# Cross-attention in 16 batches: the 64-row products of two batches in one row, sums ahead of additions, Wq loaded and turned in halves

## The chip, the cores and the metric

The kernel runs on one core of one Trainium2 chip. The metric is the device time of one execution in microseconds (us). The kernel before has a median of 275.02 us in 3 runs (274.48 to 275.05).

## The reference

One cross-attention layer with 8 heads of width 256, all in float32: 16 batches of 256 rows of `x` (256 wide) attend to 77 rows of a context (192 wide), and a residual and a layer norm follow.

```python
Q = (x @ Wq), K = (c @ Wk), V = (c @ Wv)      # each split into 8 heads of 256
score = einsum('bhqd,bhkd->bhqk', Q, K) / sqrt(256)
score = where(mask, score, -inf)
attn = softmax(score)
ctx = einsum('bhqk,bhkd->bqhd', attn, V).reshape(B, 256, 8 * 256)
out = ctx @ Wo + x
return (out - mean(out)) * rsqrt(var(out) + 1e-5) * gamma + beta
```

## The kernel before

**Algebra.** Nothing of size Q, K or V is formed. A prologue works out, for each head, `g = Wk Wq^T / 16` (tiles gA, gB) and `u = Wv Wo` (uA, uB). Then a batch needs `a = g^T c^T` (so that the scores are `x a`) and `vw = c u` (so that the output is the sum over heads of attn times vw).

**128 rows and 64 rows.** The context is 192 wide, so each of these products is a sum over 128 rows (part A, operands cA, gA, uA) and over 64 rows (part B, operands cB, gB, uB, in which two 64-row products run side by side). `prepare_a` (line 153) and `prepare_vw` (line 198) return three functions: part_A and part_B, which issue matmuls into the same PSUM tiles, part A with start and part B with stop, and copies, a list of what is then to be copied to SBUF. prepare_a makes, in each step, one pair of heads of the a of a *group* of four batches (the next group's); prepare_vw makes the vw of one batch. In the last group the a is made in halves of two batches, spread over the steps of batches 10 to 13.

**PSUM.** All tiles come from one pool of eight slots (ps_mm, tag mm), a slot being a bank. A new tile waits, at its first matmul, for the last reader of the tile whose slot it takes.

**The order.** The schedule is manual: each engine executes its instructions in the order in which the program issues them. The loop from line 882 runs over b = -1 to 14; its body makes the scores and softmax of batch b + 1 (*new*, two tiles of 128 rows), the attention output of batch b (*now*) and the layer norm of batch b - 1 (*old*). I call it "the step of batch b + 1". In the steps up to batch 13 it issues:

- TensorE: scores of the two new tiles (L283, 4 banks); part A of vw and of a (L208, L173), then part B of both (L219, L185), 2 + 4 banks; the products of the batch before (`seven`, L416, banks pm and po), a seven-product scheme of Strassen's kind over two tiles and two halves of the columns.
- Vector engine: for each new tile two additions of the bias (s, L298) and the maximum (top, L305); up to batch 6 a turn of vr (L273); for each tile the old tile's statistics (L471, L474), the softmax sum and its reciprocal (den, L318, L320); normalise of the old tiles (L513, L532) around the transposes of p (L336) and, in two steps of four, of the next group's x (L150); the two additions of po to the output (L463, in `add_seven`).
- Scalar engine: eight exponentials for each tile (L312), two small instructions of the layer norm (L492, L493), the copies of vw and a (L922), the copy of pm to m (L439).
- GpSimd: p = e times the reciprocal, two instructions per tile (L326); the differences of vw blocks for the next `seven` (L379); `add_seven`'s five additions (L449); the four sums of p blocks for the next `seven` (`sums`, L396 to L399).

The first step (b = -1) has no now and no old, and has a bias for the batches from 4 on to prepare on the Vector engine and GpSimd. The last two steps use plain products (`attend`, L348) in place of seven.

**The prologue.** SP issues all loads of weights in order. `load_blocks` (line 574) loads a block tile with four DMAs, one for each 32 partitions. Wk and Wq of head pairs 1 to 3 come alternately, then Wv, Wo and the rest of the context. `turn_blk` (line 677) transposes a pair's two blocks on the Vector engine in 32 by 32 blocks (L679), `g_of_pair` (L777) and `rest_of_g_of_pair` (L793) multiply them.

Of the kernel before, what the change touches and what calls it, by code (L numbers as in the profile page):

```python
# [8 lines left out]
F32 = mybir.dt.float32  # L9
# [6 lines left out]
P = 128  # L16
# [3 lines left out]
GB = 4  # L20
# [5 lines left out]
def kernel(  # L26
# [13 lines left out]
    nc = tc.nc  # L40
    B, S, DI = x.shape
# [3 lines left out]
    NG = B // GB  # L45
# [3 lines left out]
    NF = H // 2  # L49
    KR = S2 - KM  # L50
    BK = 32
    NM = P // BK
# [97 lines left out]
        nc.vector.transpose(cols, cols)  # L150


    def prepare_a(g, places, lo=0, hi=GB):


        if 0 in places:
            a_of[g] = in_two("a", [P, 2, GB, H, S2], g)
        parts = [
            (2 * u + i, dc) for u in places for dc in range(2) for i in range(2)
        ]  # L160
        batches = slice(g * GB + lo, g * GB + hi)
        banks = [
            ps_mm.tile([P, hi - lo, S2], F32, tag="mm", name=f"pa_{g}_{h}_{dc}_{lo}")
            for h, dc in parts
        ]

        def cols(dc, i):
            return slice((2 * i + dc) * BK, (2 * i + dc + 1) * BK)

        def part_A():  # L170
            for (h, dc), o in zip(parts, banks):
                for i in range(NM):
                    nc.tensor.matmul(  # L173
                        flat(o[i * BK : (i + 1) * BK]),
                        gA[:, h, cols(dc, i)],
                        flat(cA[:, batches, :]),
                        start=True,
                        stop=False,
                    )

        def part_B():
            for j in range(0, len(parts), 2):
                for i in range(NM):
                    for k, (h, dc) in enumerate(parts[j : j + 2]):
                        nc.tensor.matmul(  # L185
                            flat(banks[j + k][i * BK : (i + 1) * BK]),
                            gB[half(k), h // 2, cols(dc, i)],
                            flat(cB[half(k), batches, :]),
                            start=False,
                            stop=True,  # L190
                        )
# [6 lines left out]
    def prepare_vw(b):  # L198

        vw_of[b] = vwp.tile([P, 4, 2, P], F32, tag="vw", name=f"vw_{b}", bufs=3)  # L200
        parts = slice(0, 4) if b < NS else slice(1, 5)
        pv = []

        def part_A():
            for k in range(2):
                pv.append(ps_mm.tile([P, 2 * DI], F32, tag="mm", name=f"pv_{b}_{k}"))
                for i in range(NM):
                    nc.tensor.matmul(  # L208
                        pv[k][i * BK : (i + 1) * BK],
                        cA[:, b, k * BK : (k + 1) * BK],  # L210
                        uA[:, parts, :, i],
                        start=True,
                        stop=False,
                    )

        def part_B():
            for i in range(NM):
                for k in range(2):
                    nc.tensor.matmul(  # L219
                        pv[k][i * BK : (i + 1) * BK],  # L220
                        cB[half(k), b, k * BK : (k + 1) * BK],
                        uB[half(k), parts, :, i],
                        start=False,
                        stop=True,
                    )
# [89 lines left out]
    def weigh(t):  # L315
        e = e_of.pop(t)
        den = st.tile([P, H], F32, tag="den", name=f"den_{t}")
        nc.vector.tensor_reduce(den, e, AX.X, ALU.add)  # L318
        rden = st.tile([P, H], F32, tag="rden", name=f"rden_{t}")
        nc.vector.reciprocal(rden, den)  # L320
        p = p_ring[t % 2]
        e_mh = e.rearrange("p (m h) k -> p m h k", h=2)
        rden_mh = rden.rearrange("p (m h) -> p m h", h=2)
        for cols, keys in ((slice(2 * KM), slice(KM)), (slice(2 * KM, 2 * S2), slice(KM, None))):
            part = p[:, :, cols].rearrange("p m (h k) -> p m h k", h=2)
            nc.gpsimd.tensor_tensor(  # L326
                part,
                e_mh[:, :, :, keys],
                rden_mh.unsqueeze(3).to_broadcast(list(part.shape)),
                ALU.mult,  # L330
            )
# [226 lines left out]
    with tc.tile_pool(name="wonce", bufs=1) as wp:  # L558
# [12 lines left out]
        wq_rows = wq[:, : 2 * D].rearrange("(t p) f -> p t f", p=P)  # L571
        wk_ends = wk[P:, : 2 * D].rearrange("r (e f) -> r e f", e=2)

        def load_blocks(to, blocks):
            for i in range(NM):
                nc.sync.dma_start(to[i * BK : (i + 1) * BK], blocks[i])


        rest = slice(first * CR, None)
# [24 lines left out]
        nc.sync.dma_start(c_sb, c_rows[:, :first, :])  # L604
        for a in range(1, NF):
            load_blocks(wk_blk[:, a - 1], wk_blocks[a])
            load_blocks(wq_blk[:, a - 1], wq_blocks[a])

        nc.scalar.preload_act_table_set("natural_log_exp_and_others")

# [64 lines left out]
            )  # L675

        def turn_blk(a):
            for blk, of in ((wk_blk, kT_blk), (wq_blk, qT_blk)):
                nc.vector.transpose(  # L679
                    of[a].rearrange("p n (m r) -> p m n r", r=BK),  # L680
                    blk[:, a - 1].rearrange("p m (n c) -> p m n c", c=BK),
                )

        def turn_c():
# [192 lines left out]
    pools[1] = vwp = late  # L877


    assert QT == 2  # L880
    last = NT - 1
    for b in range(-1, B - 1):
        old = range(max(b - 1, 0) * QT, b * QT)
        now = range(max(b, 0) * QT, (b + 1) * QT)
        new = range((b + 1) * QT, (b + 2) * QT)
        for t in new:
            scores(t)
        if b == B - 2:
# [12 lines left out]
        if g < NG - 1 or g == NG - 1 and n < NF // 2:  # L901
            work.append(prepare_a(g, (n,)))
        elif b < NS:
            work.append(prepare_a(NG - 1, (NF // 2 + n % 2,), *((0, 2) if g < NG else (2, GB))))
        for part_A, _, _ in work:
            part_A()
        for _, part_B, _ in work:
            part_B()
        for i, t in enumerate(new):
            exponential(t)  # L910
            if old and b < B - 2:
                finish(old[i])
            weigh(t)
        if old and b < B - 2:
            spread(old[0], old[-1] + 1)
        if b < 0:
            bias_of(GB, B)
            for j in range(GT // 2, GT, 2):
                transpose_x(0, j)
        for _, _, copies in work:  # L920
            for dst, src in copies():
                nc.scalar.copy(dst, src)  # L922
        if b + 1 < NS:
            differences(b + 1)
        if b < NS:
            if now:
                seven(b)
            if old:
                invert(old[0], old[-1] + 1)
                normalise(old[0])  # L930
            for t in new:
                turn(t)
            if g < NG and n >= NF - 2:
                for j in range((n - NF + 2) * GT // 2, (n - NF + 3) * GT // 2, 2):
                    transpose_x(g, j)
            if old:
                normalise(old[1])


            if g < NG and n == NF - 1:  # L940
# [80 lines left out]
```

## Time and profile before

| What | Value |
|---|---|
| median of 3 runs | 275.02 us (274.48 to 275.05) |
| the profiled execution | 274.61 us, of which its span 272.8 us |
| busy TensorE | 97% of the span |
| busy Vector engine / GpSimd / Scalar engine | 78% / 62% / 50% |
| granted TensorE clock | 0.999 |
| chain that ended last | TensorE 89%, DMA 7%, Vector engine 1%, SP's queue 1% |

The span is the time between the first and the last instruction of the profiled execution. PE is TensorE's matmuls, DVE the Vector engine, ACT the Scalar engine, POOL GpSimd, SPq the queue that issues DMAs. A line of the chain has the start, the time it takes in the chain, the engine, the tile and the source line. A line of an engine's timeline has the start, the time from the first start to the last end, the line, the operation, output <- input, shapes, the number of instructions and, in brackets, how long the engine was idle before and what ended that. An instruction's time can overlap the one before it by some hundredths.

### The profile page before, as it was taken

To read this page: it belongs to the slowest core of one execution; us is meant where nothing else is said; L and a number is where in the kernel's file an instruction comes from. 1 tells how busy PE (TensorE), PEld (TensorE's weight loads), DVE (VectorE), ACT (ScalarE), POOL (GpSimd) and SP (SyncE) were. 2 spreads that over 40 slices of the span, in tenths; PEclk is the share of its full clock that TensorE was granted. 3 is DMA by queue.
4 is the path that set the end of the run, shared out by engine and by line. 5 is a ranking of instruction groups with operands and counts; after the bars stand their busy time and mean duration, and the time that the engine had idled before them with its cause. 6 is when DMAs were issued, how large, how long until landed. Compare 5 with 4: busy or idle time off the path is not lost.

```text
span 272.8 us, 14124 instructions
## 1 busy us (share of the span) xinstructions
PE 265.8 (97%) x6312; PEld 194.3 (71%) x6312; DVE 214.1 (78%) x418; ACT 136.2 (50%) x444; POOL 170.4 (62%) x231
## 2 busy tenths in 40 slices
PE   7999999999999999999999999999999999999992
PEld 6557486867494949495959586867796969694662
DVE  0554938589759898979799897878798989889875
ACT  3233225363918182827364646464546372927652
POOL 1000002809887878687878777777788789845754
PEclk9999999999999999999999999999999999999999
DMA  6999989940000322310221405000504061010102
GB/s 191 194 198 189 305 160 183 278 53 2 2 5 4 88 35 73 124 44 4 70 52 36 87 19 180 31 16 9 116 2 120 2 197 41 5 43 4 61 22 77
DMA packets 42460, 22.66 MB, mean 83 GB/s; under 512 B 23632, under 2 KB 41632, under 8 KB 42400
## 3 DMA queue, kind: packets, MB, share of 16 engines
q1 hardware_dynamic: 42400, 21.77, 34.8%
q8 instruction: 49, 0.80, 1.3%
q14 instruction: 11, 0.09, 0.1%
HBM read 17.57 MB, written 4.19 MB: 80 GB/s over the span
## 4 chain that ended last, share of the span: by engine, by line
PE 89%; DMA 7%; DVE 1%; SPq 1%; issue 0%; DVEq 0%
PE ps L283 25%; PE pa L173 11%; PE po L416 10%; PE pv L208 10%; PE pm L416 9%; PE pv L219 6%; PE pa L185 5%; DMA wq_blk<-in_L_xattn_Wq_dram 5%; PE po L348 4%; PE pu L717 3%; PE pr L242 2%; DMA c_sb<-in_ctx_dram 2%; PE pw L731 1%; PE pr L254 1%; PE po L364 1%; PE pgb L777 1%
## 5 line engine op out<-in xcount | busy, mean ns | idle before, releaser
L312 ACT ACTIVATE e<-s,top 128x77 f32<-128x77 f32 x256 | 66.8, 346 | 73.4 <-DVE top L305 73.4
L283 PE MATMUL ps<-a,xT 128*32 128x154 f32 x2048 | 70.0, 294 | 0.0
L326 POOL TENSOR_TENSOR p<-e,rden 128x512 f32<-128x512 f32 x64 | 47.8, 768 | 31.8 <-DVE rden L320 16.6
L283 PEld LDWEIGHTS ps<-a,xT 128*32 128x32 f32 x2048 | 66.0, 110 | 1.5 <-issue 0.8
L298 DVE TENSOR_TENSOR s<-ps,bias 128x308 f32<-128x308 f32 x64 | 29.7, 473 | 14.7 <-PE ps L283 14.6
L449 POOL TENSOR_TENSOR xg<-xg,m 128x256 f32<-128x256 f32 x39 | 28.6, 733 | 12.8 <-DVE xg L463 10.7
L173 PE MATMUL pa<-cA,gA 128*32 128x308 f32 (+1 forms) x576 | 36.4, 394 | 0.0
L173 PEld LDWEIGHTS pa<-cA,gA 128*32 128x32 f32 x576 | 18.4, 110 | 20.3 <-issue 9.1
L208 PE MATMUL pv<-uA,cA 128*32 128x512 f32 x256 | 30.4, 592 | 0.0
L318 DVE TENSOR_REDUCE den<-e 128x8 f32<-128x616 f32 x32 | 24.9, 777 | 5.1 <-ACT e L312 4.9
L305 DVE TENSOR_REDUCE top<-s 128x8 f32<-128x616 f32 x32 | 25.4, 795 | 1.1
L336 DVE STREAM_TRANSPOSE pT<-p 128x640 f32<-128x640 f32 x32 | 25.1, 813 | 0.9 <-POOL p L326 0.9
L379 POOL TENSOR_TENSOR ts<-vw 128x768 f32<-128x768 f32 x13 | 23.9, 1839 | 0.0
L532 DVE SCALAR_TENSOR_TENSOR xg<-xg,rstd,bet 128x256 f32<-128x256 f32 x26 | 20.9, 803 | 1.9
L185 PE MATMUL pa<-cB,gB 64*32 64x308 f32 (+1 forms) x576 | 20.3, 392 | 0.0
L922 ACT COPY vw<-pv 128x512 f32<-128x512 f32 x32 | 17.1, 584 | 6.3 <-PE pv L219 6.3
L185 PEld LDWEIGHTS pa<-cB,gB 64*32 64x32 f32 x576 | 10.7, 107 | 12.3 <-issue 9.2
L594 POOL COPY cRA<-cA 128x208 f32<-128x208 f32 x1 | 0.4, 358 | 29.8 <-DVE cA L593 29.8
L416 PE MATMUL po<-vr,pT 128*32 128x128 f32 x416 | 18.5, 273 | 0.0
L922 ACT COPY a<-pa 128x308 f32<-128x308 f32 (+1 forms) x56 | 17.5, 416 | 0.0
L219 PE MATMUL pv<-uB,cB 64*32 64x512 f32 x256 | 17.4, 601 | 0.0
L463 DVE TENSOR_TENSOR xg<-po,xg 128x256 f32<-128x256 f32 x31 | 11.7, 415 | 5.0 <-PE po L416 4.6
(117 smaller groups left out, 408.7 us busy)
## 6 DMA issues: line engine op xcount, KB each, us to landing
xT<-in_x_dram SPq DMA_DIRECT2D x32, 128.0 KB, 4.4
xg<-in_x_dram SPq DMA_DIRECT2D x4, 1024.0 KB, 6.7
out_dram<-xg SPq DMA_DIRECT2D x11, 256.0 KB, 2.8
wo<-in_L_xattn_Wo_dram SPq DMA_DIRECT2D x4, 512.0 KB, 6.2
wq_blk<-in_L_xattn_Wq_dram SPq DMA_DIRECT2D x12, 128.0 KB, 4.7
wvT<-in_L_xattn_Wv_dram SPq DMA_DIRECT2D x16, 96.0 KB, 3.6
out_dram<-xg SPq DMA_DIRECT2D x10, 128.0 KB, 1.7
wk_blk<-in_L_xattn_Wk_dram SPq DMA_DIRECT2D x12, 96.0 KB, 4.6
```

The costliest lines, as they stand in the source:

```text
L173: nc.tensor.matmul(flat(o[i * BK : (i + 1) * BK]), gA[:, h, cols(dc, i)], flat(cA[:, batches, :]), start=True, stop=False,)
L185: nc.tensor.matmul(flat(banks[j + k][i * BK : (i + 1) * BK]), gB[half(k), h // 2, cols(dc, i)], flat(cB[half(k), batches, :]), start=False ...
L208: nc.tensor.matmul(pv[k][i * BK : (i + 1) * BK], cA[:, b, k * BK : (k + 1) * BK], uA[:, parts, :, i], start=True, stop=False,)
L219: nc.tensor.matmul(pv[k][i * BK : (i + 1) * BK], cB[half(k), b, k * BK : (k + 1) * BK], uB[half(k), parts, :, i], start=False, stop=True,)
L283: nc.tensor.matmul(ps[m // 2][i * BK : (i + 1) * BK, m % 2 * 2 * S2 : (m % 2 + 1) * 2 * S2], xT_of[g][:, j * NM + m, dc], flat(a_of[g][:, ...
L298: nc.vector.tensor_tensor(s[:, a * H // 2 : (a + 1) * H // 2], ps[a][:, : H // 2 * S2].rearrange("p (h k) -> p h k", k=S2), bias[:, b, :]. ...
L305: nc.vector.tensor_reduce(top, s, AX.X, ALU.max, negate=True)
L312: nc.scalar.activation(e[:, h], s[:, h], AF.Exp, bias=top[:, h : h + 1])
L326: nc.gpsimd.tensor_tensor(part, e_mh[:, :, :, keys], rden_mh.unsqueeze(3).to_broadcast(list(part.shape)), ALU.mult,)
L416: nc.tensor.matmul(out[i * BK : (i + 1) * BK], weight[:, i], moving, start=(n == 0), stop=(n == len(terms) - 1),)
L449: nc.gpsimd.tensor_tensor(to, to, what, ALU.add)
L922: nc.scalar.copy(dst, src)
```

## The change

1. `prepare_a` and `prepare_vw` take `rest_first`. With it part B has start and part A has stop, so part B can be issued first. The two pv tiles of prepare_vw are now allocated when it is called, ahead of prepare_a's tiles.
2. In the steps of batches 0, 2, 4, 6, 8 and 10 TensorE gets the products of this batch and of the next: part A, part B (this batch), part B, part A (next batch). The steps of batches 1, 3, ..., 11 have none. The Scalar engine copies the first set between the exponentials of the two tiles and the second after both. From batch 12 on (`alone`) each step has its own products, with the copies after both tiles' exponentials, as before.
3. In these even steps GpSimd's four sums come ahead of add_seven's additions; elsewhere after them, as before.
4. The three Wq blocks are loaded in two halves each (8 DMAs of 64 KB in place of 4 of 128 KB) and transposed in two instructions in place of one.

```diff
@@ prepare_a (prepare_vw has the same start and stop) @@
-    def prepare_a(g, places, lo=0, hi=GB):
+    def prepare_a(g, places, lo=0, hi=GB, rest_first=False):
...
-                        start=True,
-                        stop=False,
+                        start=not rest_first,
+                        stop=rest_first,
...
-                            start=False,
-                            stop=True,
+                            start=rest_first,
+                            stop=not rest_first,
@@ prepare_vw @@
-        pv = []
+        pv = [ps_mm.tile([P, 2 * DI], F32, tag="mm", name=f"pv_{b}_{k}") for k in range(2)]
@@ loads @@
-        def load_blocks(to, blocks):
-            for i in range(NM):
-                nc.sync.dma_start(to[i * BK : (i + 1) * BK], blocks[i])
+        def load_blocks(to, blocks, parts=1):
+            n = to.shape[1] // parts
+            for m in range(0, parts * n, n):
+                for i in range(NM):
+                    nc.sync.dma_start(
+                        to[i * BK : (i + 1) * BK, m : m + n], blocks[i][:, m : m + n]
+                    )
...
-            load_blocks(wq_blk[:, a - 1], wq_blocks[a])
+            load_blocks(wq_blk[:, a - 1], wq_blocks[a], parts=2)
@@ turn_blk @@
-            for blk, of in ((wk_blk, kT_blk), (wq_blk, qT_blk)):
+            half_q = DI // BK // 2
+            for blk, of, rows in (
+                (wk_blk, kT_blk, slice(0, NL)),
+                (wq_blk, qT_blk, slice(0, half_q)),
+                (wq_blk, qT_blk, slice(half_q, None)),
+            ):
                 nc.vector.transpose(
-                    of[a].rearrange("p n (m r) -> p m n r", r=BK),
-                    blk[:, a - 1].rearrange("p m (n c) -> p m n c", c=BK),
+                    of[a].rearrange("p n (m r) -> p m n r", r=BK)[:, rows],
+                    blk[:, a - 1, rows].rearrange("p m (n c) -> p m n c", c=BK),
                 )
@@ loop @@
+    def work_of(b, rest_first=False):
+        g, n = b // GB + 1, b % GB
+        work = [prepare_vw(b, rest_first)]
+        if g < NG - 1 or g == NG - 1 and n < NF // 2:
+            work.append(prepare_a(g, (n,), rest_first=rest_first))
+        elif b <= NS:
+            part = (0, 2) if g < NG else (2, GB)
+            work.append(prepare_a(NG - 1, (NF // 2 + n % 2,), *part, rest_first))
+        return work
+
+    def copy_out(work):
+        for _, _, copies in work:
+            for dst, src in copies():
+                nc.scalar.copy(dst, src)
...
-        work = [prepare_vw(b + 1)]
...
-        for part_A, _, _ in work:
+        alone = b + 1 >= B - GB
+        works = work_of(b + 1) if alone or n % 2 == 0 else []
+        for part_A, _, _ in works:
             part_A()
-        for _, part_B, _ in work:
+        for _, part_B, _ in works:
             part_B()
         for i, t in enumerate(new):
             exponential(t)
             if old and b < B - 2:
                 finish(old[i])
             weigh(t)
+            if i == 0 and works and not alone:
+                copy_out(works)
+                works = work_of(b + 2, rest_first=True)
+                for _, part_B, _ in works:
+                    part_B()
+                for part_A, _, _ in works:
+                    part_A()
...
-        for _, _, copies in work:
-            for dst, src in copies():
-                nc.scalar.copy(dst, src)
+        copy_out(works)
...
+            ahead = works and not alone
+            if ahead:
+                sums(b + 1)
             if now:
                 add_seven(b)
-            if b + 1 < NS:
+            if b + 1 < NS and not ahead:
                 sums(b + 1)
```

More of the change, by code (lines that the diff above doesn't have):

```diff
@@ L196, in prepare_a, with prepare_vw @@
         return part_A, part_B, copies
-    def prepare_vw(b):
+    def prepare_vw(b, rest_first=False):
         vw_of[b] = vwp.tile([P, 4, 2, P], F32, tag="vw", name=f"vw_{b}", bufs=3)
         parts = slice(0, 4) if b < NS else slice(1, 5)
-        pv = []
+        pv = [ps_mm.tile([P, 2 * DI], F32, tag="mm", name=f"pv_{b}_{k}") for k in range(2)]
         def part_A():
             for k in range(2):
-                pv.append(ps_mm.tile([P, 2 * DI], F32, tag="mm", name=f"pv_{b}_{k}"))
                 for i in range(NM):
@@ L211, in part_A @@
                         uA[:, parts, :, i],
-                        start=True,
-                        stop=False,
+                        start=not rest_first,
+                        stop=rest_first,
                     )
@@ L222, in part_B @@
                         uB[half(k), parts, :, i],
-                        start=False,
-                        stop=True,
+                        start=rest_first,
+                        stop=not rest_first,
                     )
@@ L899 @@
         g, n = (b + 1) // GB + 1, (b + 1) % GB
-        work = [prepare_vw(b + 1)]
[L901 to L904, printed above, removed]
-        for part_A, _, _ in work:
+        alone = b + 1 >= B - GB
+        works = work_of(b + 1) if alone or n % 2 == 0 else []
+        for part_A, _, _ in works:
             part_A()
-        for _, part_B, _ in work:
+        for _, part_B, _ in works:
             part_B()
```

## The prediction

> **What bounds the kernel now.** I read the engines' shares first, then the chain of waits, then the engines' timelines step by step. The first line says that TensorE is full; the chain says where.
>
> ```profile
> PE 265.8 (97%) x6312; PEld 194.3 (71%) x6312; DVE 214.1 (78%) x418; ACT 136.2 (50%) x444; POOL 170.4 (62%) x231
> ```
> ```profile
> 18.07 4.58 DMA wq_blk<-in_L_xattn_Wq_dram
> ...
> 22.77 1.26 DVE qT L679
> ...
> 24.17 2.00 PE pgb L777 x16
> ...
> 91.85 4.19 PE ps L283 x128
> 96.04 1.72 PE pv L208 x16
> 97.75 2.07 PE pa L173 x32
> 99.83 1.02 PE pv L219 x16
> 100.85 1.04 PE pa L185 x32
> 101.88 1.88 PE pm L416 x64
> 103.77 2.18 PE po L416 x80
> 105.95 4.19 PE ps L283 x128
> ```
>
> From 24.17 to 268 us the chain lies on TensorE without a hole. A batch is one step of 14.10 us: scores 4.19, the 128-row products (part A) 3.79, the 64-row ones (part B) 2.06, the seven products 4.06. So whatever shortens TensorE's row shortens the kernel, as long as the other engines keep up. The Vector engine's row of batch 3's step shows how closely they do: it starts 1.3 us after the scores and ends with the next step's scores already running.
>
> ```profile
> 92.97 0.48 DVE L298 TENSOR_TENSOR s<-ps,bias 128x308 f32<-128x308 f32 x1 [0.29 <-PE ps L283]
> ...
> 101.38 1.09 DVE L532 SCALAR_TENSOR_TENSOR xg<-xg,rstd,bet 128x256 f32<-128x256 f32 x1
> ...
> 105.54 0.56 DVE L532 SCALAR_TENSOR_TENSOR xg<-xg,rstd,bet 128x256 f32<-128x256 f32 x1
> 106.02 0.75 DVE L463 TENSOR_TENSOR xg<-po,xg 128x256 f32<-128x256 f32 x2
> ```
>
> The first step has no seven products and more GpSimd work; this is GpSimd's row there:
>
> ```profile
> 61.31 3.11 POOL L326 TENSOR_TENSOR p<-e,rden 128x512 f32<-128x512 f32 x4 [7.62 <-ACT e L312]
> ...
> 66.65 1.83 POOL L379 TENSOR_TENSOR ts<-vw 128x768 f32<-128x768 f32 x1
> 68.43 0.74 POOL L396 TENSOR_TENSOR ss<-pT 128x256 f32<-128x256 f32 x1
> ```
>
> **What the Trainium skill says.** "TensorEngine Tiling (Array Packing)", Key Properties: "Changing tiling mode (not just tile) drains the TensorE". The trace agrees: 16 part B matmuls of pv run twice as many at once as the 16 of part A (1.72 us), so they should take 0.86, and take 1.02; the 64 of pm take 1.88 where 80 like them take 2.18, so 1.74. A turn costs 0.14 to 0.16 us. "PSUM — Partial Sum Buffer", Specifications: 8 banks. The pool here has eight slots, so every ninth tile waits for the reader of the first. "SBUF — State Buffer", Who interferes with whom: a Vector instruction with two SBUF inputs contends with a GpSimd one that reads SBUF. The two L532 above agree: 1.09 beside GpSimd's work, 0.56 (and 0.48 elsewhere) without. "DMA: Bandwidth & Descriptors", Specifications: line rate from 512 B; the halves of Wq keep 512-byte rows, so bytes per second need not fall.
>
> **The change, part by part.** Call the step of an even batch up to 10 double (it now has the products of two batches), that of an odd one short.
>
> *Turns.* A pair had four turns (A to B, B to seven, twice), 0.60 us; now A to B and, in the second set, B to A, 0.30. Six pairs: **-1.8**. The new turn B to A is in no row; I take 0.15, bounds 0 and 0.25 (all that a step takes beyond its streams, 14.10 less 13.6, over two turns). Bounds of the part: -0.9 and -3.0.
>
> *The short step and the Vector engine.* A short step takes TensorE 4.19 + 3.90 = 8.1 us; a double one 19.8. The Vector engine's work per batch stays. In batch 3's step its last instruction ends at 106.02 + 0.66 = 106.68, 15.0 after the scores began (91.67 in the timeline). With 8.1 us of TensorE it ends D = 6.9 after the next scores begin, not 0.9. Likewise D = 6.2 for batch 5 (no xT turn), 6.7 for batch 7, 6.1 for batch 9.
>
> *The copies ahead of the second exponential.* In the double step the Scalar engine does tile 0's eight exponentials, the copies of set 1, tile 1's exponentials, then the copies of set 2. From the Vector engine's restart at D: two s at 0.43 apart and the maximum put the first exponential at D + 1.78 (207.06 against 205.28, where the step of batch 11 started late), eight of them end at D + 3.84, two vw copies at D + 4.9, two pa copies at D + 5.6, seen by TensorE at D + 5.7. TensorE, unhindered, is through scores, A and B at 10.04, through set 2's pv part B at 10.9, and needs at 11.4 the banks that the first two pa copies free (a double step takes 18 banks). So it waits D - 5.7: **1.2, 0.5, 1.0** in the double steps of batches 4, 6 and 8. In batch 2's it waits for nothing: batch 1 has no older batch to normalise, D is about 2.8. Batch 10's sets are shorter (pa of 154 columns), the need comes at 9.7, the copies at D + 5.4 = 11.5: **1.9**. Queued behind the waiting matmul are the whole of set 2 and the seven products, and all who wait for those. In the double step itself the Vector engine idles until tile 1's exponentials (13.7 to 15.2), then has 6.2 to 6.8 us left; that ends at about 21, where a short step's first s is due. So lateness doesn't pile up.
>
> *First pair.* Set 1's copies end at 64.9, as now; tile 1's exponentials, now over at 61.2, run 64.9 to 67.0. Behind them: den and reciprocal (1.0), GpSimd's p of tile 1 to 69.6, bias 72.0, differences 73.9, and the third sum, which the second product reads, at 76.1. TensorE gets there after 15.9 (scores and both sets), 4.19 and 0.44 from 53.3: 73.8. Wait **2.3**; today the sums are ready in time. The cover is gone because this step has no seven products.
>
> *Sums ahead of the additions* cost nothing: in a double step they follow the differences at about 19 and end at 22 to 23; the short step needs them at 24.4 or later. What waits behind them, add_seven, ends some 5 us into the short step, before the Vector engine's statistics at 6.3. Without this edit those sums would end near 26 and be late.
>
> *After the pairs.* Batch 12's step (the old order) starts with D = 6.8: its third and fourth pa banks wait for the s of its tile 0: **1.1**; batch 13's first score bank for a vw copy: **0.2**. From there the Vector engine stays about 3 us later than today, as a step (12.6) exceeds its row (12.0) by 0.6 only. The last transposes now end 1.4 us before TensorE needs the first: **1.5**.
>
> *Wq in halves.* Twelve more loads on SP's queue, and the wvT, wo, cA and xT loads behind them. A load waits for the one eight before it (8.08 follows c_sb's landing at 8.07), and unhindered SP issues one each 0.42 to 0.49 us (12 of Wq take 7.1 with waits). Now loads land every 0.44 (96 KB) to 0.6 us (128 KB), so the DMA engines set the pace; with 64 KB halves SP does. The last Wq load is then issued at 20.1 to 21.6 instead of 18.07 and lands some 2.85 later (96 KB lands in 3.1 when little is queued), 23.0 to 24.4 instead of 22.65. Against that only half is left to turn, 0.65 instead of 1.26. TensorE starts the third pair at 23.8 to 25.2, today 24.17; it can't win more than the 0.51 it idles there. I take **+0.4**, bounds -0.5 and +1.1. Six Vector instructions instead of three cost nothing elsewhere: the first two pairs' are due when TensorE is still on the products before. wvT has 2 us to spare, wo about 1.
>
> *Sum.* -1.8 + 0.4 + 2.3 + 4.6 + 1.3 + 1.5 = +8.3. The profiled execution took 274.6 (span 272.8 and 1.8 around it), 0.4 below the median of the runs: 282.9, slower by 3%.
>
> **Rivals.**
> 1. *The Vector engine is quicker.* For: GpSimd now works at other times, and its collisions cost 0.6 (L532) and 0.46 (L513) per step; without them D falls by 1.1. Against: its products run at the same point of the short step. The pairs' waits become 0.1, 0, 0 and 0.8, the end 0.6; the first pair's stays: 274.6 - 1.8 + 0.4 + 2.3 + 0.9 + 0.6 = 277.0.
> 2. *Faster: turns are dearer than the matmul rows say.* Place: the weight loads ahead of part B and of pm, idle 0.50 each. Price: up to 0.25 a turn, 3.0 in all. Point: it decides once all waits sum to less than that, which means D below 5.7 and only the first pair's 2.3 left: 274.6 - 3.0 + 2.3 - 0.3 = 273.6. Against: today's rows of pv and pm.
> 3. *Waits feed each other*: SP at its late end (+1.1), lateness at the end not absorbed (4 instead of 1.5), one more us in the pairs: 287.
>
> **How the numbers follow.** Forecast (279.5 to 286.5): 0.62. Rival 1 (275.2 to 279.5): 0.19. Rival 2 (below 274.5): 0.10. Rival 3 (above 286.5): 0.06. No change (within 0.2%, about what a measurement of this kernel can tell): 0.03. Leaving out rivals 2 and 3 and little else, the range is 275.2 to 286.5. Faster 0.11, same 0.04, slower 0.85.
>
> **What would show it.** Right: a hole in TensorE's row before pm's second product of batch 0 of about 2.3 us; holes before set 2's pa part B in the double steps of batches 4, 6, 8 and 10, released by the Scalar engine's copies; the Vector engine's first s in these steps 6 to 7 us after the scores' start; TensorE's third pair near 24.6. Each double step's turns: two, of 0.15. Wrong: TensorE without holes from batch 0 to 11; or an end of the Vector engine's row in short steps before 13.8 us after their scores.

## The result, and the profile after

The changed kernel takes 288.59 us (median of 6 runs, 286.45 to 289.88) against 274.56 (6 runs, 274.12 to 275.05): 1.050 times as long, with an interval of 1.046 to 1.054. The forecast was 282.9 with a range up to 286.5. Slower was right, the size was not. The profiled execution is the fastest of the six, 286.45 (span 284.7), so 11.8 above the profiled 274.61 of before where the sum of the prediction said 8.3. Stage by stage, from the starts of the scores in TensorE's row of both profiles (the double steps are those of even batches):

| Stage | Forecast | Measured |
|---|---|---|
| up to the scores of batch 0 (53.27 before, 57.39 after) | +0.4 | **+4.1** |
| batches 0 and 1 | 2.3 - 0.3 = +2.0 | +2.0 |
| batches 2 and 3 | -0.3 | 0.0 |
| batches 4 and 5 | 1.2 - 0.3 = +0.9 | +0.6 |
| batches 6 and 7 | 0.5 - 0.3 = +0.2 | 0.0 |
| batches 8 and 9 | 1.0 - 0.3 = +0.7 | +0.6 |
| batches 10 and 11 | 1.9 - 0.3 = +1.6 | +1.5 |
| batch 12 | +1.1 | **+2.4** |
| batch 13 | +0.2 | +0.2 |
| batch 14 to the end | +1.5 | +0.5 |

The loop as a whole came out as forecast to the tenth (7.9 and 7.8), but that is luck: the errors at batch 12 (1.3 too little) and at the end (1.0 too much) nearly cancel. The prologue did not. Batch 3's step is 0.26 longer in this profile than in experiments 2 and 12, where batches 2 and 3 gain the forecast 0.3; what held it here is not known.

The shares of the engines in the changed kernel, first line of the page:

```profile
PE 269.3 (95%) x6312; PEld 198.4 (70%) x6312; DVE 213.6 (75%) x421; ACT 133.6 (47%) x444; POOL 169.7 (60%) x231
```

TensorE still has the largest share, but it is no longer the chain. Before, the chain lay on it from 24 us on without a hole; now only 27% of the chain is TensorE's, 29% is the Vector engine's, 15% the Scalar engine's. These are its pieces after the change (start, time, engine, tile, line):

```profile
14.09 1.32 SPq L577
...
20.24 0.44 SPq L577
21.20 1.31 SPq L577
23.51 0.44 SPq L577
...
28.84 3.16 DMA wvT<-in_L_xattn_Wv_dram
...
35.52 3.60 SPq L590
39.16 5.39 DMA cA<-in_ctx_dram
...
45.03 0.83 DVE cA L596
...
50.95 0.57 PE pr L241 x4
...
67.64 1.40 ACT a L901 x4
69.04 1.98 ACT e L311 x8
...
76.13 1.80 POOL ts L378
...
79.36 0.74 POOL ss L397
80.14 1.52 PE pm L415 x48
...
118.03 0.68 DVE xg L462 x2
118.84 1.76 PE pa L173 x24
```

Up to 50 us the chain is SP, which issues loads (L577 and L590), and what these loads bring. From there on it enters TensorE's row at the holes. TensorE's timeline shows them, with the time that it idled and who ended that in the brackets:

```profile
26.20 2.00 PE L785 MATMUL pgb<-qT,kT 64*128 64x256 f32 x16 [1.94 <-DVE qT L687]
...
36.14 7.57 PE L725 MATMUL pu<-wo,wv_turned 64*128 64x256 f32 x64 [0.39 <-DMA wo<-in_L_xattn_Wo_dram]
...
50.95 0.57 PE L241 MATMUL pr<-cRA,uA 128*64 128x208 f32 x4 [1.01 <-DVE uB L866]
...
80.14 0.65 PE L415 MATMUL pm<-vw,ss 128*32 128x128 f32 x16 [2.07 <-POOL ss L397]
...
118.84 1.76 PE L173 MATMUL pa<-cA,gA 128*32 128x308 f32 x24 [0.22 <-DVE xg L462]
...
123.31 1.56 PE L185 MATMUL pa<-cB,gB 64*32 64x308 f32 x32
...
235.57 0.64 PE L415 MATMUL pm<-vw,ss 128*32 128x128 f32 x16 [0.90 <-POOL ss L397]
```

The Vector engine's row across the end of batch 3's step and the start of batch 4's (whose scores start at 111.9) answers to the one shown of batch 3 before:

```profile
113.16 1.09 DVE L531 SCALAR_TENSOR_TENSOR xg<-xg,rstd,bet 128x256 f32<-128x256 f32 x1
...
117.54 0.49 DVE L531 SCALAR_TENSOR_TENSOR xg<-xg,rstd,bet 128x256 f32<-128x256 f32 x1
117.94 0.75 DVE L462 TENSOR_TENSOR xg<-po,xg 128x256 f32<-128x256 f32 x2
118.61 0.85 DVE L297 TENSOR_TENSOR s<-ps,bias 128x308 f32<-128x308 f32 x2
```

Its first s comes 6.7 after the scores (forecast 6.9), in batch 6 6.2 (6.2), in batch 10 5.9 (6.1). The two L531 are 1.09 and 0.49 long, as before. And GpSimd in the first step, where p of tile 1 now starts at 72.22 and the third sum follows the bias and the differences:

```profile
72.22 1.60 POOL L325 TENSOR_TENSOR p<-e,rden 128x512 f32<-128x512 f32 x2 [5.42 <-DVE rden L319]
...
74.39 1.73 POOL L553 TENSOR_TENSOR bias<-bias,nan 128x924 f32<-128x924 f32 x1
76.08 1.84 POOL L378 TENSOR_TENSOR ts<-vw 128x768 f32<-128x768 f32 x1
...
79.36 0.73 POOL L397 TENSOR_TENSOR ss<-pT,ss 128x256 f32<-128x256 f32 x1
```

**The theory now.** The prologue's loss is SP's: twelve more loads are twelve more issues, whatever their size, and all later loads come that much later. The loop's loss is what the prediction said. The rivals: the late prologue is chance or belongs to the longer loop; small loads are slow loads; and in the loop, other waits than those named.

### The profile page after: what moved, and what is told of

The parts are those of the page before. It is cut to its first block, busy times and chain, and to the rows that moved or that the text cites. A ratio compares the mean times of both kernels' runs of the same rounds, so it can differ in the third digit from the quotient of the medians.

```text
span 284.7 us, 14154 instructions
## 1 busy us (share of the span) xinstructions
PE 269.3 (95%) x6312; PEld 198.4 (70%) x6312; DVE 213.6 (75%) x421; ACT 133.6 (47%) x444; POOL 169.7 (60%) x231
## 4 chain that ended last, share of the span: by engine, by line
DVE 29%; PE 27%; ACT 15%; SPq 9%; POOL 8%; DMA 5%; issue 4%; DVEq 0%; POOLq 0%; ACTq 0%
ACT e L311 13%; PE ps L282 7%; SPq L577 7%; PE pa L173 5%; DVE pT L335 4%; DVE den L317 4%; DVE xg L531 4%; DVE xg L512 3%; PE pv L207 3%; PE po L415 3%; PE pa L185 3%; DVE top L304 3%; PE pm L415 2%; PE pv L218 2%; DVE xg L462 2%
## 5 line engine op out<-in xcount | busy, mean ns | idle before, releaser
L282 PEld LDWEIGHTS ps<-a,xT 128*32 128x32 f32 x2048 | 66.7, 110 | 1.1 <-issue 0.3
L173 PE MATMUL pa<-cA,gA 128*32 128x308 f32 (+1 forms) x576 | 37.9, 395 | 1.2 <-DVE xg L462 1.2
L297 DVE TENSOR_TENSOR s<-ps,bias 128x308 f32<-128x308 f32 x64 | 28.4, 469 | 6.4 <-PE ps L282 6.3
L207 PE MATMUL pv<-uA,cA 128*32 128x512 f32 x256 | 31.1, 594 | 0.0
L531 DVE SCALAR_TENSOR_TENSOR xg<-xg,rstd,bet 128x256 f32<-128x256 f32 x26 | 21.8, 840 | 2.2 <-DVE xg L512 0.5
L185 PE MATMUL pa<-cB,gB 64*32 64x308 f32 (+1 forms) x576 | 21.8, 394 | 0.6 <-ACT vw L901 0.6
L207 PEld LDWEIGHTS pv<-uA,cA 128*32 128x32 f32 x256 | 9.0, 110 | 11.6 <-issue 9.9
```

What stands on the lines that cost most here:

```text
L173: nc.tensor.matmul(flat(o[i * BK : (i + 1) * BK]), gA[:, h, cols(dc, i)], flat(cA[:, batches, :]), start=not rest_first, stop=rest_first,)
L185: nc.tensor.matmul(flat(banks[j + k][i * BK : (i + 1) * BK]), gB[half(k), h // 2, cols(dc, i)], flat(cB[half(k), batches, :]), start=rest_ ...
L207: nc.tensor.matmul(pv[k][i * BK : (i + 1) * BK], cA[:, b, k * BK : (k + 1) * BK], uA[:, parts, :, i], start=not rest_first, stop=rest_first,)
L282: nc.tensor.matmul(ps[m // 2][i * BK : (i + 1) * BK, m % 2 * 2 * S2 : (m % 2 + 1) * 2 * S2], xT_of[g][:, j * NM + m, dc], flat(a_of[g][:, ...
L531: nc.vector.scalar_tensor_tensor(y, y, rstd, bet, ALU.mult, ALU.add)
```

## Experiments: the halves of Wq

Times are medians; ratios are to the kernel before, run on the same chip, with their intervals.

**1. Halves alone.** The kernel before with this part of the change and nothing else:

```diff
-            load_blocks(wq_blk[:, a - 1], wq_blocks[a])
+            load_blocks(wq_blk[:, a - 1], wq_blocks[a], parts=2)
```

(and `load_blocks` and `turn_blk` of the change.)

> The kernel before with Wq of three pairs loaded and turned in halves, and nothing else. Theory (SP can issue one load in 0.48 us whatever its size, so twelve more loads push every later load back): the scores of batch 0 start about 4 us later than before (57.3 instead of 53.3), the loop takes what it takes before, 278.3 to 279.0 in all. Rival (the halves cost the 0.4 that was forecast, and the rest of the late prologue is the luck of one profile or comes from the new loop's longer program): 274.8 to 275.3.

279.18 us (278.24 to 279.76), ratio 1.016 (1.013 to 1.019). The scores of batch 0 start at 56.80, 3.5 later than before, and each step of batches 0 to 14 takes what it took before, to 0.01. So the loss is the halves', not chance and not the loop's. The third pair waits 2.26 for its turned Wq and starts 1.9 late; half a clock behind that wait (see 12) stretches its products by the other 1.6. Half a clock is not needed for the loss: the other three runs, at a clock of 0.999 or 1.000, took longer (278.82 to 279.76) than the profiled one (278.24, at 0.993).

**2. Products alone.** The changed kernel with `load_blocks` and `turn_blk` of before:

```diff
-            load_blocks(wq_blk[:, a - 1], wq_blocks[a], parts=2)
+            load_blocks(wq_blk[:, a - 1], wq_blocks[a])
```

> The changed kernel with Wq loaded and turned whole, as before: only the products in pairs, their copies and the sums ahead are left. Theory: the scores of batch 0 start where they start before (53.3, within 0.6), the loop takes 7.8 more, so about 282.4. Rival (the late prologue has nothing to do with the halves): about 286, scores at 57.

282.78 us (281.66 to 284.27), ratio 1.030 (1.026 to 1.034); scores of batch 0 at 53.35. The two parts add up: 4.7 for the halves and 8.3 for the products are 13.1, the whole change 14.0 (13.5 when it was run again, in 12).

**3. Turns in halves, loads whole.**

```diff
-            for blk, of in ((wk_blk, kT_blk), (wq_blk, qT_blk)):
+            half_q = DI // BK // 2
+            for blk, of, rows in (
+                (wk_blk, kT_blk, slice(0, NL)),
+                (wq_blk, qT_blk, slice(0, half_q)),
+                (wq_blk, qT_blk, slice(half_q, None)),
+            ):
```

> The kernel before with whole loads, but each Wq block turned by two Vector instructions of half the size. Theory (loads alone cost): 274.6, within 0.5; the third pair starts at 24.1 to 24.3. Rival (the turn in two instructions costs by itself, by an instruction's start-up or its place in the Vector engine's row): 275.2 or more, with the prologue's later steps behind by as much.

274.43 us in 20 runs, ratio 1.000 (0.999 to 1.001). More Vector instructions cost nothing, as the prediction said. In its profile the third pair even starts at 23.72 without a wait and the scores of batch 0 0.4 earlier than before; then batch 0's step takes 1.0 more than before, in part in an idle time of TensorE that no wait explains. No gain is left in the medians.

**4. Whole loads and twelve tiny ones.** This tells the number of loads from their size:

```diff
             load_blocks(wq_blk[:, a - 1], wq_blocks[a])
+            for i in range(NM):
+                nc.sync.dma_start(
+                    tiny[i * BK : (i + 1) * BK, a], wq_blocks[a][i][:, 0, :BK]
+                )
```

> The kernel before with whole loads and turns, and four loads of 128 bytes a partition (4 KB each) after each Wq block, into a tile that nothing reads: twelve loads more with hardly more bytes. It computes the same as before. Theory (each load costs SP its issue): nearly as late as with halves, the scores of batch 0 at 56 to 57.5, 277.5 to 279. Rival (the halves cost because smaller loads move fewer bytes per second): within 0.5 of before, since the large loads are whole.

280.13 us (279.55 to 281.41), ratio 1.021 (1.019 to 1.024); scores of batch 0 at 58.28. It is slower than the theory's number, and no faster than with halves: the third pair waits 3.09, and its products, at half the clock behind that wait (see 12), take 3.78 instead of 2.00. Of the 5.0 by which the scores are late, 2.3 are there when the third pair starts and 2.7 come from half a clock. The queue that issues shows why the loads come late. The columns are the start, the time from the first issue to the end of the last, line, tile and number of loads. The kernel before:

```profile
16.00 2.39 SPq L576 DMA_DIRECT2D wq_blk<-in_L_xattn_Wq_dram  x4
18.46 8.73 SPq L576 DMA_DIRECT2D wvT<-in_L_xattn_Wv_dram  x16
27.24 3.81 SPq L620 DMA_DIRECT2D wo<-in_L_xattn_Wo_dram  x4
```

The same queue in the changed kernel:

```profile
18.80 4.66 SPq L577 DMA_DIRECT2D wq_blk<-in_L_xattn_Wq_dram  x8
23.51 8.78 SPq L577 DMA_DIRECT2D wvT<-in_L_xattn_Wv_dram  x16
32.33 1.87 SPq L623 DMA_DIRECT2D wo<-in_L_xattn_Wo_dram  x4
```

And with whole and tiny loads:

```profile
19.48 2.60 SPq L577 DMA_DIRECT2D wq_blk<-in_L_xattn_Wq_dram  x4
22.12 1.84 SPq L610 DMA_DIRECT2D tiny<-in_L_xattn_Wq_dram  x4
24.00 7.68 SPq L577 DMA_DIRECT2D wvT<-in_L_xattn_Wv_dram  x16
```

Four tiny loads of 4 KB take SP 1.84, four whole ones of 96 or 128 KB 1.9 where nothing holds them up: about 0.48 a load, whatever it carries. wvT and wo follow some 5 us later than before in both kernels, the context (cA) some 3 us. The number of loads is what counts.

**5. Second halves on GpSimd's queue.** From here on `load_blocks` of the halves, with

```diff
-                    nc.sync.dma_start(
+                    (nc.gpsimd if m else nc.sync).dma_start(
```

> The kernel before with Wq in halves, where the second halves (twelve loads) are issued by GpSimd's queue, which is idle in the prologue up to 10.5 us, and the first halves by SP's as before: SP has as many loads as the kernel before. Theory (the halves cost because SP issues them): the scores of batch 0 start within 1 us of before's 53.3, about 274 to 275.5. Rival (64 KB loads cost, whoever issues them): 277.5 to 279, as with the halves on one queue.

277.98 us (276.90 to 280.02), ratio 1.014 (1.009 to 1.019): between both. In the profile the third pair and all behind it wait for nothing, as the theory says, but the *first* pair waits 1.7 for its Wq: GpSimd's loads land 6.3 after their issue, SP's halves 4.3 (medians). That is not GpSimd's queue as such. SP's own four loads of Wk issued between 4.0 and 5.5 us land 6.1 to 6.8 later here, 4.4 to 4.5 in the kernel before, and GpSimd's four loads of the same time land 6.2 to 7.0 later: early loads of both queues are in flight together and all land later. Scores of batch 0 at 54.99. The remedy brought a wait of its own, so this alone doesn't decide.

**6. Only the third pair's second halves there.**

```diff
-            load_blocks(wq_blk[:, a - 1], wq_blocks[a], parts=2)
+            load_blocks(wq_blk[:, a - 1], wq_blocks[a], parts=1 + a // (NF - 1))
```

> The kernel before with only the third pair's Wq loaded in halves, its second halves (four loads) issued by GpSimd's queue at the start, all turns of Wq in halves: SP has as many loads as before. Theory (SP's issues cost, not the size of a load; GpSimd's queue cost the first pair its wait, which is not there now): the third pair's products start at 23.7 to 24.2, scores of batch 0 at 52.5 to 53.4, 273.9 to 274.7. Rival (64 KB loads cost, whoever issues them): 1 or more above before.

275.96 us in 15 runs (274.98 to 277.68), ratio 1.005 (1.003 to 1.007): neither number. The scores of batch 0 start at 54.74, 1.5 late. That lateness is there from the beginning: TensorE waits 0.7 and 0.8 for the first weights (wq_nat, wk_last), which now share the DMA engines with GpSimd's four early loads, and the first pair starts at 16.09 instead of 14.10. After it nothing waits for a load any more: the third pair starts at 25.64 right behind the products before it, pu and pr without a hole. The four 64 KB loads of SP land 2.5 to 3.5 after their issue, its whole ones 4.8 in the block before. So size does not make a load late here. What can be had by a better order of queues stays open; none of these kernels beats the one before.

## Experiments: the products in pairs

They start from the products alone (2); the holes in its TensorE row are these (who waited for whom, us in total, times, longest):

```profile
PE pm L415 <- POOL ss L397: 2.9, 2, 2.1
PE pa L173 <- DVE xg L462: 2.0, 3, 0.9
...
PE pa L185 <- ACT vw L892: 0.6, 1, 0.6
```

The pair of batches 2 and 3 has no wait and takes 27.89 where it took 28.20: the saved turns are 0.31 a pair, forecast 0.30.

**7. Batches 0 and 1 apart.**

```diff
-        alone = b + 1 >= B - GB
+        alone = b + 1 >= B - GB or b + 1 < 2
```

> The products in pairs without the halves of Wq, with batches 0 and 1 apart as before (their products in their own steps, sums after the additions). Theory (the first pair's wait of 2.05 for GpSimd's third sum goes, its saved turns of 0.3 go too): 1.7 to 2.0 less than with all pairs, about 280.5 to 281; the steps of batches 2 to 15 as with all pairs. Rival (that wait is hidden lateness, which comes back in the next pair): within 0.7 of the kernel with all pairs.

280.23 us (279.84 to 280.85), ratio 1.020 (1.015 to 1.025), 2.5 less than 2 (theory 1.7 to 2.0). In the profiles the first pair takes 24.29 instead of 26.26 and all other stages of the loop the same within 0.1. That wait stands by itself.

**8. Copies of set 1 behind both exponentials.**

```diff
-            if i == 0 and works and not alone:
-                copy_out(works)
...
+        if works and not alone:
+            copy_out(works)
```

> The products in pairs without the halves of Wq, with the copies of set 1 (and set 2 after them) behind the exponentials of both tiles. Theory of the prediction (TensorE's waits in the double steps are for these copies, 2.1 later now; the first pair's sums are early enough): first pair 2.05 less, the double steps of batches 4, 6, 8 and 10 each 1.5 to 2.1 more, 4 to 6 in all more than the kernel with all pairs, 286 to 288. Rival (the waits in the double steps come from the Vector engine's last additions of the step before, which hold the third bank of pa in set 1; the copies have room): 2 less, about 280.

288.36 us (288.00 to 288.64), ratio 1.049 (1.044 to 1.054), 5.6 more than 2. The first pair takes 23.99: its wait is gone and its turns saved. The pairs from batch 4 on take 2.0, 2.0, 2.0 and 3.5 more. Of the 3.5, 2.0 are wait; the other 1.5 come from half a clock behind it, from 209.3 to 212.7 us (see 12). TensorE's waits in this kernel:

```profile
PE pa L185 <- ACT vw L892: 6.9, 4, 2.6
...
PE pa L173 <- DVE xg L462: 1.2, 3, 0.6
```

Four waits for the copies, in place of one. So the place of the copies sets both waits, against each other, as the mechanism of the prediction says.

**9. Less work for the Vector engine.** One multiplication in the layer norm left out in each short step:

```diff
-                normalise(old[0])
+                normalise(old[0], scaled=alone or n % 2 == 0)
```

> The products in pairs without the halves of Wq; in the steps of batches 3, 5, 7, 9 and 11 the first old tile's multiplication by rstd and addition of beta on the Vector engine is left out (1.1 of that engine's time in each, so that layer norm of five tiles is not finished). Theory (the waits in the double steps and in batch 12's are the Vector engine's lateness, D less some 5.7): each of those waits shrinks by up to 1.1, first pair as it is: 3 to 4.5 less than with the whole work, 277.5 to 279.5. Rival (the waits are TensorE's turns, GpSimd's sums or the Scalar engine's own order): less than 1 gained.

280.53 us (279.49 to 282.22), ratio 1.021 (1.015 to 1.028), 2.3 less than 2: between both theories. The profile shows the mechanism in batches 4 and 8: in batch 4 the first s comes 6.4 after the scores instead of 7.0, and the pair of 4 and 5 takes 0.64 less; that of 8 and 9 also 0.64 less, the 28.20 of before. In batch 10 the pair gains 0.2 only: the first s still comes 5.7 after the scores instead of 5.9, since the second transpose of p now waits 0.52 for GpSimd's p, and one normalise beside GpSimd takes 1.26 instead of 0.89. D is the Vector engine's lateness up to there, and GpSimd's next.

**10. Sums behind the additions.**

```diff
-            ahead = works and not alone
+            ahead = False
```

> The products in pairs without the halves of Wq, with GpSimd's four sums after the additions in the double steps too, as in the kernel before. Theory (in a double step the additions wait for TensorE's last product, so the sums come some 2.5 to 3 later than now and the second product of each short step waits for them): 1 to 2.5 more in each of the short steps of batches 3 to 11, at most partly made up in the next double step, 285 to 291. Rival (the place of the sums is of no account): within 0.7.

282.29 us (281.74 to 283.62), ratio 1.026 (1.021 to 1.032): no dearer than 2. The theory's number falls. Its waits:

```profile
PE pm L415 <- POOL ss L397: 5.9, 6, 2.1
```

The short steps do wait for the sums, as expected: those of batches 3, 5, 7 and 9 take 8.85 to 8.87 instead of 8.11, that of batch 11 takes 10.07. But the waits for xg and vw are gone from the list, and batch 12's step takes 13.05 instead of 15.16. A longer short step gives the Vector engine the time it lacks, and the step behind it waits that much less. Pair 8 and 9 takes 28.84 with the sums ahead and 28.84 with them behind.

**11. Sums ahead in batch 11's step too**, with batches 0 and 1 apart:

```diff
-            ahead = works and not alone
+            ahead = works and not alone or b + 1 == B - GB - 1
```

> The products in pairs from batch 2 on without the halves of Wq, with GpSimd's sums ahead of its additions in batch 11's step too. Theory (TensorE's wait for the third sum in batch 12's step, 0.9 and 1.2 with the turn around it, goes, and the additions are not missed): 0.9 to 1.3 less than with batches 0 and 1 apart alone, about 279. Rival (in that step the sums wait for the Vector engine's transposes and hold up the additions, the statistics and so the Vector engine): the same or more, the wait moved to the step of batch 12 or 13.

280.67 us (279.41 to 281.82), ratio 1.024 (1.021 to 1.027), against 280.23 without: nothing gained. The wait for the sum is gone from the list, and this is in it:

```profile
PE pa L173 <- DVE xg L462: 1.8, 3, 1.0
...
PE po L415 <- issue: 1.1, 1, 1.1
```

The second is a new hole of 1.1 in the same seven products of batch 12's step (15.27 long, 15.24 without this edit). "issue" means that no wait explains it. The trace has a load of 16 KB of instructions from 229.5 to 230.6 us, and TensorE stands from 230.7 to 231.8; that it had run out of instructions is likely, not shown. The 16 profiles of this document have six such holes of TensorE, of 0.2 to 1.1, and each begins 0.1 to 1.3 after the end of such a load.

## Experiments: the clock

The other five runs of the changed kernel took 1.4 to 3.4 more than the profiled one and had a mean TensorE clock of 0.986 to 0.988, the profiled one 0.999.

**12. The changed kernel again**, unedited, to find the low stretch.

> The changed kernel once more, to find where its other runs lose 1.5 to 3.4 us against the profiled one. Theory (a pause of TensorE of 2 us or more, as the third pair's at 24 us and the first pair's at 78, is in some executions followed by some microseconds in which its clock is granted at half): 286.5 to 290, and if this profile's mean clock is below 0.995, its low stretch lies behind one of these two pauses. Rival (the loss is spread over the run, or lies in loads that come later): no such stretch, or one elsewhere.

287.73 us (286.64 to 288.50), ratio 1.048 (1.044 to 1.052). This profile caught it, at 0.988. A table of stretches (from:to and length, then the busy time and number of instructions of PE, its weight loads, DVE, ACT and POOL; the column ahead of the last two is TensorE's clock):

```profile
77.00:79.00 2.00, 1.39 (x48) 1.12 (x36) 1.97 (x5) 0.60 (x3) 2.00 (x3) 1.00 0.00 0
79.00:81.00 2.00, 0.55 (x20) 0.56 (x24) 1.93 (x4) 2.00 (x10) 1.84 (x3) 1.00 0.00 0
81.00:83.00 2.00, 2.00 (x60) 2.00 (x56) 1.00 (x3) 1.97 (x8) 1.49 (x3) 0.70 0.00 0
83.00:85.00 2.00, 2.00 (x47) 2.00 (x43) 1.24 (x3) 0.00 (x0) 1.38 (x3) 0.50 0.03 8
85.00:87.00 2.00, 2.00 (x68) 1.99 (x64) 1.59 (x4) 0.00 (x0) 2.00 (x3) 0.95 0.00 0
```

The pause for the sum ends at 80.45. From 81.8 to 85.2 the clock is at half, 3.4 us, and batch 1's step takes 12.05 instead of 10.39. The other stretch lies behind the third pair's wait, there 2.81: the pair's products take 3.38 instead of 2.00. The Trainium skill, "TensorE: Matmul & The Clock Gate", in "HAM oscillation — how this bites in real kernels", has such a clock at half behind idle gaps beyond about 3.4 us. The half clock is there, but here gaps of 2.06 and 2.81 were enough, in some executions.

**13. Both pauses filled** in the changed kernel, and **14. the first pair's pause filled** in the products alone:

```diff
+    def fill(n):
+        spare = ps_mm.tile([P, P], F32, tag="mm", name=f"spare_{n}")
+        for _ in range(n):
+            nc.tensor.transpose(spare, ident, ident)
...
         contract(pm[:, 0], *block(pT[0][:, 0:2], b11))
+        if b == 0:
+            fill(8)
```

(13 has `fill(7)` ahead of the third pair as well; 14 has `fill(16)` and no other.)

> The changed kernel with transposes of the identity matrix, that nothing reads, in TensorE's two long pauses: seven ahead of the third pair's products, eight ahead of the second product of batch 0 (0.22 each, so 1.5 and 1.8 of pauses of 1.9 and 2.1). Theory (the pauses bring the half clock): the mean clock is 0.995 or more in all runs and the median 1.5 to 2 below that of the changed kernel, 286 to 287. Rival (the clock has nothing to do with pauses): the median within 0.5 of the changed kernel's, the clock about 0.987 again.

287.86 us (287.65 to 288.50), ratio 1.049 (1.047 to 1.052): the clock is up, at 0.994 to 0.998 in all four runs, and the time is not down. The seven transposes took 0.99 and left 2.10 of the third pair's pause. Half a clock behind the third pair costs little in these kernels in any case: with it (12) the scores of batch 0 start at 57.70, without it at 57.39 in the first profile and at 57.91 here, where TensorE waits for wo and the context instead.

> The products in pairs without the halves of Wq, with sixteen transposes of the identity matrix, that nothing reads, in TensorE's pause ahead of the second product of batch 0 (at 0.11 each about 1.8 of the 2.05). Theory (the pause is followed in some executions by half the clock, which costs 1.7 each time): no run below a mean clock of 0.996, median 1 to 1.5 below the 282.8 of the same kernel without them, 281.3 to 281.8. Rival (the other runs' longer times come from elsewhere): median within 0.4 of 282.8.

282.41 us (282.18 to 282.95), ratio 1.028 (1.026 to 1.031). The clock is 0.996 or 0.997 in all, the two long runs of 283.45 and 284.27 have no like here, but the median is 0.4 below the unfilled one's: the rival's number. In the profiles of both kernels the pair of batches 8 and 9 takes 0.5 to 0.8 more than without the transposes, and both list an idle time named "issue" (0.3 and 0.6); the added instructions may have moved the points at which TensorE waits for its instructions, which I did not test. So half a clock behind a pause, and its price of 1.5 to 1.7 (2.7 in 4), is shown in the profiles that caught it (first pair: 9, 10 and 12; third pair: 1, 4 and 12; batch 10's wait of 2.59: 8). That it makes the other long executions is likely from their mean clock, and why filling the first pair's pause does not pay in the median stays open. It is 2 us of 14.

## Why the prediction was wrong, step by step

**Wq in halves: the failed step.** "The last Wq load is then issued at 20.1 to 21.6 instead of 18.07 [...] I take **+0.4**, bounds -0.5 and +1.1." It was issued at 23.0 and landed at 25.3 (forecast 23.0 to 24.4); the scores started 4.1 late, 3.5 with the halves alone. That SP sets the pace was right: from the second pair's Wk on it issued a load every 0.48, and 36 loads at that pace from the first Wk on (4.00) would put the last one at 20.8, inside the forecast. Two terms were put at nothing.

First, SP's stops. Two issues of this stretch took 1.3 instead of 0.43 (at 14.09 and 21.20, both in the chain above), and loads of the first pair were held up by another 0.5. Both stops lie beside a load of 16 KB of instructions; so does every issue of Wk, Wq, Wv and Wo that took more than 0.8, in all 16 profiles. The kernel before had such a stop too (1.45 at 14.51), but its Wq loads landed 4.6 to 4.8 after their issue, so that the DMA engines still had several queued. Now the last ones land 2.2 after theirs, and each stop delays all that follow. So the third pair started 2.0 late (24.17 to 26.20) instead of 0.4.

Secondly, and more: I stopped at the third pair. "wvT has 2 us to spare, wo about 1" was on record one line further down, but SP was 5 us late with wvT and wo and 3.5 with the last load of cA. pu waited for wo (0.4, and 0.4 inside it), and cA landed at 44.55 instead of 39.43, so that the Vector engine's turn of it and the copies of uB behind it held pr (1.2). 2.0 + 0.9 + 1.2 is the 4.1. Where half a clock stretched the third pair's products (1 and 4), TensorE came to wo and cA later and did not wait for them.

**Turns.** Right: 0.31 a pair measured in 2.

**First pair.** Right in place, cause and size: 2.2 from start to start against 2.3, gone in 7 and in 8.

**Double steps.** The sizes were right (pairs within 0.3), the place only in part. In batches 4 and 8 half or more of the wait comes earlier, at the second bank of set 1's pa. A short step takes six banks, so this bank is the po of the step before, which the Vector engine's last additions (L462) still read. It is the same lateness D, met 6.4 after the scores instead of 11.4. In batch 10 most of the wait is where I had it, at set 2's pa part B. The pair of 10 and 11 lost 1.5 and had saved 0.3 in turns, so its waits came to 1.8 (forecast 1.9); with the products alone (2) they came to 1.5. A check of the slots one by one would have shown both.

**Sums ahead.** "Without this edit those sums would end near 26 and be late": they are late (10), and it costs nothing: the short steps wait for the sums, and the double steps and batch 12 wait that much less for the Vector engine.

**Batch 12.** 2.4 instead of 1.1. The 1.1 is there, but at the second pa bank, which the last additions (L462) hold, and not at the third and fourth. Missed was the third sum of batch 11: that step is short and has the additions ahead of the sums, and batch 12's step has only one set of products before it needs them. I had asked of the sums in double steps only. **The end**: 1.5 forecast, 0.5 measured. I had the Vector engine stay 3 late; its first s comes 1.8 later after the scores than before in batch 13 and 1.1 in batch 14. That batch 12's longer wait used up the rest is my reading and was not tested.

**Rivals.** The quicker Vector engine (277.0) is refuted by D, which came as forecast; the dearer turns (273.6) by 0.31 a pair. The third, waits that feed each other, gave 287 and is nearest by number, but not by its mechanism: only SP's part of it happened, at nearly four times the price (4.1 for 1.1), and the loop's waits replaced each other.

## What to carry to other kernels

Count the loads, not the bytes: when a queue issues back to back, every added load delays all later ones by its issue time, so follow the lateness to the last load of the queue and not only to the one that was split. When TensorE's work is moved between steps and another engine's is not, the waits are set by that engine's lateness; list the banks in order to see where it is met first, and expect that removing one such wait uncovers the next.

## What the runs showed of the hardware

- SP issues a load about every 0.48 us when nothing holds it up, for 4 KB, 64 KB, 96 KB and 128 KB alike. Up to wo, single issues took 0.9 to 2.3 us, and each of these, in all 16 profiles, lies beside a load of 16 KB of instructions.
- After pauses of TensorE of 2.06 to 3.09 us its clock was at half for 3.4 us in some executions (6.8 in experiment 4), which stretched the work by 1.5 to 1.7 us (2.7 in 4). After pauses of 2.05 (experiment 2), 2.07 (the changed kernel) and 2.10 (13) it was not.
- When GpSimd's queue issued early loads beside SP's (experiment 5), loads issued between 4.0 and 5.6 us landed 6.1 to 7.0 us later on both queues; SP's loads of that time landed 4.4 to 4.5 us later in the kernel before.
